# A convolution and mixture-of-experts kernel: the first tile's chain, the fillers, and the place of a conditional

## The chip, the cores and the metric

The kernel runs on one core of a Trainium2 chip. The metric is the device time of one execution in microseconds (us). A core has five engines that run their own instruction streams and wait for each other by semaphores: TensorE (PE, with its weight loads PEld), VectorE (DVE), ScalarE (ACT), GpSimd (POOL) and SyncE (SP), which here only issues transfers. Transfers by DMA run beside them.

## The reference

The input `x` has 8 x 256 tokens of 512 elements. Two stages follow, each with a residual:

```python
def _L0_xattn_ref(v, k, bias, x1, x2, num_heads):      # v = layernorm(x); x1 = x2 = ctx
    vr, x1r, x2r = (a.reshape(B, H, 8, L) for a in (v, x1, x2))         # H = 32
    kv = vr[:, :, :, None, :] * x2r[:, :, None, :, :]
    y = irfft(rfft(kv, n=2 * L) * rfft(k, n=2 * L), n=2 * L)[..., :L]   # causal convolution by head
    y = y + kv * skip
    return einsum('bhijl,bhil->bhjl', y, x1r).reshape(B, D, L)

x = x + _L0_xattn_ref(layernorm(x), ...)
x = x + ffn(layernorm(x))      # shared expert of 704, and the best 2 of 8 experts of 352
```

All of it is in float32. `ffn` is a gated network: `silu(x @ wg.T) * (x @ wu.T) @ wd.T`, for every token with the shared weights, and for each token with its two picked experts, weighted by their scores.

## The kernel before

**Convolution.** Tokens are laid out as 16 tiles of 128 rows (8 batches by 16 rows), two heads to a tile, 32 heads in all. For each head POOL forms the products `kv` in four blocks of 128x512 (`make_kv`), PE convolves them with the head's Toeplitz matrix (`conv_products`), and DVE weighs and sums the result. Each tile's rows are first normed and transposed (`vT`), later tiles a long way ahead through memory. Tiles 0 and 1 have no time for that: `first_of_all` norms them on the spot and `make_vT` transposes them on PE, whence ACT copies them out of PSUM. While tile 0's data are on their way, PE multiplies a block of zeros (`filler`, 128x256, `WARM` times); the result isn't used.

The chain of tile 0 before its first convolution is thus: `x` lands; DVE takes mean and variance; ACT the root (which needs the constant `eps`, written by POOL at L240); DVE the reciprocal and the product of mean and reciprocal; ACT the norm; PE four transposes; ACT one copy; POOL the first `kv` block; PE. ACT must load a table of function values before its first root. At L425 the first head takes `kv[:, 0]` three times before it needs the other blocks.

The order of the work is written out by hand in the program; each engine runs its instructions in the order in which they stand there. A loop over the heads (L892) makes one head's `kv` two heads ahead, and steps of the shared expert are spread over the later heads.

**Experts.** Routed tokens are sorted into blocks of 128 rows, each of one expert. There can be up to `NBLK` = 39 blocks; `NSURE` = 36 are always run, and the last three only if the count `more`, which the kernel itself computes and every engine loads into a register, exceeds 36. With these inputs it doesn't. For a block `k`: POOL gathers the rows (`gather`, four indirect DMAs), DVE transposes them (`block_T`), PE multiplies them by the gate and up weights (`block_up`), ACT and DVE form the hidden rows, DVE transposes these in 16 pieces (`block_hT`), PE multiplies by the down weights (`block_down`), ACT scales, and POOL adds the rows into the output with an indirect DMA. Each such scatter waits until the one before has landed, since two may add into the same row. PE reads the block's expert number into a register (`load_ek`, L1040). In `blocks`, gathers run four blocks ahead, the transposed rows two, and `block_down` two behind. The last block's hidden rows are transposed on PE (`last_hT`).

The conditional (`tc.If`, L1190) comes after all 36 blocks. Each engine has a compare and branch there. On the way that is not taken into the body an engine waits until it has finished what it was given, and moves its semaphores on by as much as the body would have; on POOL this also means a wait for all of its DMAs and an instruction INC_SWDGE_SEM.

Of the kernel before, what the change touches and what calls it, by code (L numbers as in the profile page):

```python
# [8 lines left out]
F32 = mybir.dt.float32  # L9
I32 = mybir.dt.int32  # L10
AF = mybir.ActivationFunctionType
ALU = mybir.AluOpType
# [45 lines left out]
H9 = 10  # L58
EPS = 1e-5
CTXBUFS, TZBUFS = 5, 3  # L60
WARM = 6
SCALE = 2.5


# [1 line left out]
def tile_xattn_moe(  # L66
# [74 lines left out]

    ones = const.tile([P, P], F32, name="ones")
    G.memset(ones, 1.0)
    filler = rows.tile([P, 2 * P], F32, tag="xg", name="filler")
    G.memset(filler, 0.0)
    ident = const.tile([P, P], F32, name="ident")
# [121 lines left out]
    def normed(xn, src, rb):  # L268
        A.activation(xn, src, AF.Identity, scale=rb[0], bias=rb[1])
# [5 lines left out]
        A.copy(dst, pt)  # L275

    vT, convT, xfT, xn1, xn2 = {}, {}, {}, {}, {}

    def make_vT(t):
        vT[t] = cvp.tile([P, NLB, B, R], F32, tag="vT", name=f"vT_{t}")  # L280
# [585 lines left out]
    def first_of_all(t):  # L866
        mv = small.tile([P, V.BN_AGGR_DIM], F32, tag="mv", name=f"mvp_{t}")
        stats(mv, f"p_{t}", x1[t])
        xn1[t] = cvp.tile([P, L], F32, tag="xn1", name=f"xn1_{t}", bufs=2)
        normed(xn1[t], x1.pop(t), rstd_of(mv, f"p_{t}"))  # L870

    first_of_all(0)

    warm = ps_acc.tile([P, 2, L], F32, tag="acc", name="warm")[:, 0, : 2 * P]
    for _ in range(WARM):
        T.matmul(warm, lhsT=ones, rhs=filler, start=True, stop=True)
    make_vT(0)
    make_kv(0)
    first_of_all(1)
    skip_products(0)  # L880
    make_kv(1)

    todo = iter(steps)
    done = 0
# [7 lines left out]
    for h in range(H):  # L892
        t, odd = divmod(h, 2)

        load_toeplitz(h + 2)
        if not odd:
            load_tile(t + 3)
            load_residual(t - 1)
        elif t == NT - 1:
            load_residual(t)  # L900
        if h == 3:
            load_shared()


        if odd and t + 2 < NT:
            first_root(t + 2)
        c, r = divmod(h - 10, 8)
        if c >= 0 and r == 2:
            route_scores(c)
        settle()  # L910
        pss = conv_products(h)
        if h > 1 and not odd:
            skip_turn(t)
        if not odd:
            first_sums(t + 2)
        elif t + 2 < NT:
            first_norm(t + 2)
            quarters(("v", t + 2), xv_d[t + 2])


        nine, picks_here = h >= H9, c >= 0 and r == 2
        if not nine:
            weigh(h, 0, pss[0])
        if odd and t > 0:
            add_residual(t - 1)
            mv = small.tile([P, V.BN_AGGR_DIM], F32, tag="mv", name=f"mv_{h}")
            stats(mv, f"2_{t}", x2[t - 1])
            rt = root(f"2_{t}", mv[:, 1:2], 1.0)
            V.reciprocal(rt, rt)
            nb = small.tile([P, 1], F32, tag="nb", name=f"nb2_{t}", bufs=3)  # L930
            V.tensor_scalar(nb, mv[:, 0:1], rt, -1.0, ALU.mult, ALU.mult)
            second_norm(t - 1, (rt, nb))
            quarters(("f", t - 1), xn_d[(t - 1) * P : t * P, :])
        if not odd and t > 0:
            add_skip(t - 1)
            if t + 1 < NT:
                square_vT(t + 1)
            if t > 1 and not picks_here:
                square_xfT(t - 2)
        if picks_here:  # L940
            route_pick(c)
        if c >= 0 and r == 4:
            route_places(c)
        if nine:
            weigh(h, 1, pss[1])
            weigh(h, 0, pss[0])
            if picks_here:
                square_xfT(t - 2)
        else:
            weigh(h, 1, pss[1])  # L950
        if odd or h == 0:
            skip_sum(t + odd)
        if h == 0:
            skip_turn(0)
        if h == 0:
            make_vT(1)

        if not odd:
            skip_spread(t)
        make_kv(h + 2)  # L960
        if not odd:
            skip_products(t + 1)

        while done < h - 9 + h // (H - 1) and steps[done][0] <= h:
            settle()
            step()

        if not odd and t > 0:
            residual_T(t - 1)
        if c >= 0:  # L970
            if r == 0:
                route_logits(c)
            if r == 1:
                route_T(c)
            if r == 3:
                route_ranks(c)
# [47 lines left out]
    def gather(k):  # L1024
        if k >= NBLK:
            return
        xgs[k] = rows.tile([P, NQ, P], F32, tag="xg", name=f"xg_{k}")
        for c in range(NQ):
            G.indirect_dma_start(  # L1029
                out=xgs[k][:, c, :],  # L1030
                out_offset=None,
                in_=xn_q,
                in_offset=bass.IndirectOffsetOnAxis(ap=src[:, c, k : k + 1], axis=0),
                bounds_check=(NTOK + P) * NQ - 1,
                oob_is_err=True,
            )
# [8 lines left out]
    def block_T(k):  # L1045

        if k >= NBLK:
            return
        xTs[k] = rows.tile([P, NLB, NQ, Q], F32, tag="xT", name=f"xT_{k}", bufs=3)
        V.transpose(  # L1050
            xTs[k].rearrange("p k c b -> p c k b"),
            xgs.pop(k).rearrange("p c (k a) -> p c k a", a=Q),
        )
# [22 lines left out]

    blk = pool("blk", 3, reuse_waits="tile")
    ps_b = pool("ps_b", 2, space=PS, reuse_waits="tile")
    NF = len(F_TILES)
    hs, hTb = {}, {}  # L1080

    def block_up(k, last):
        n = min(k + 1, NEXP)
        ps = ps_b.tile([P, 2, L], F32, tag="up", name=f"up_{k}")
        wk = wgu_sb[:, :n].rearrange("p e f -> p (e f)")
        for m in range(2):
            for j in range(NLB):
                T.matmul(  # L1088
                    ps[:, m, :FF],
                    lhsT=xTs[k][:, j].rearrange("p c b -> p (c b)"),  # L1090
                    rhs=wk[:, bass.ds(eks[k] * NGU + (m * NLB + j) * FF, FF)],
                    start=(j == 0),
                    stop=(j == NLB - 1),
                )
        hk = blk.tile([P, FF], F32, tag="h", name=f"h_{k}")
        A.activation(hk, ps[:, 0, :FF], AF.Sigmoid)  # L1096
        V.tensor_tensor(hk, hk, ps[:, 0, :FF], ALU.mult)  # L1097
        xTs.pop(k)
        if not last:
            V.tensor_tensor(hk, hk, ps[:, 1, :FF], ALU.mult)  # L1100
            hs[k] = hk
            return

        hp = blk.tile([P, NF, NQ, Q], F32, tag="hp", name=f"hp_{k}", bufs=1)
        for q0, q1, n in ((0, NQ - 1, NF), (NQ - 1, NQ, NF - 1)):
            squares = slice(q0 * NF * Q, (q0 * NF + (q1 - q0) * n) * Q)
            V.tensor_tensor(
                hp[:, :n, q0:q1].rearrange("p t q a -> p q t a"),
                hk[:, squares].rearrange("p (q t a) -> p q t a", t=n, a=Q),
                ps[:, 1, squares].rearrange("p (q t a) -> p q t a", t=n, a=Q),  # L1110
                ALU.mult,
            )
        hs[k] = hp
# [11 lines left out]
    def block_hT(k):  # L1125

        hk = hs.pop(k)
        hT = blk.tile([P, NF, NQ, Q], F32, tag="hT", name=f"hTb_{k}")
        for c in range(NQ):
            for q in range(NQ):  # L1130
                n = min(NF, FF // Q - q * NF)
# [7 lines left out]

    def block_down(k):  # L1140
        n = min(k + 1, NEXP)
        ps = ps_b.tile([P, L], F32, tag="dn", name=f"y_{k}")
        wk = wd_sb[:, :n].rearrange("p e f -> p (e f)")
        hT = hTb.pop(k)
        for ft, (_, fw) in enumerate(F_TILES):
# [4 lines left out]
                start=(ft == 0),  # L1150
                stop=(ft == NF - 1),
            )
        y = blk.tile([P, L], F32, tag="y", name=f"ys_{k}", bufs=3)
        A.activation(y, ps, AF.Copy, scale=gate[:, k : k + 1])  # L1154
        G.indirect_dma_start(  # L1155
            out=out,
# [5 lines left out]
            compute_op=ALU.add,  # L1162
        )

    def blocks(first, end):
        for k in range(first, end):
            if k + AHEAD < end:
                load_ek(k + AHEAD)
                if k > first:
                    block_T(k + AHEAD)  # L1170
            if k + AHEAD + 2 < end:
                gather(k + AHEAD + 2)
            if k < end - 1:
                block_up(k, False)
                block_hT(k)
                if k - 2 >= first:
                    block_down(k - 2)
            else:
                block_down(k - 2)
                block_up(k, True)  # L1180
                block_down(k - 1)
                last_hT(k)
                block_down(k)

    more = nc.values_load(
        used[0:1, 0:1], min_val=NEXP, max_val=NBLK,
        skip_runtime_bounds_check_because="the rows fill at most so many blocks",
    )
    blocks(0, NSURE)
    with tc.If(more > NSURE):  # L1190
        for k in range(NSURE, NBLK):
            gather(k)
        for k in range(NSURE, NBLK):
            block_T(k)
            if k < NSURE + AHEAD:
                load_ek(k)
        blocks(NSURE, NBLK)


def _orders():  # L1200
# [85 lines left out]
```

## Time and profile before

| | us |
|---|---|
| three runs: median (lowest to highest) | 799.49 (794.74 to 799.99) |
| the profiled execution | 795.8 |
| its span, first to last instruction | 794.1 |
| busy in the span: PE / DVE / POOL / ACT | 767.9 / 535.3 / 472.6 / 203.1 |
| a block of the expert loop on PE: up and down product | 4.90 and 2.74, 7.31 apart |
| last PE instruction ends | 777.2 |
| last scatter is issued | 781.3 |

The profile shows one execution. An engine is busy while an instruction of its own is at work; waits, register work and branches don't count. Names such as `kv<-vT,ctxT` give what an instruction writes and reads, `x4` says how many are merged into a line, and the bracket tells how long the engine stood idle before and who ended that. The granted clock of PE is a share of full speed. Matmuls of float32 are two passes each, so they are counted twice.

### The profile page before, as it was taken

To read this page: it belongs to the slowest core of one execution; us is meant where nothing else is said; L and a number is where in the kernel's file an instruction comes from. 1 tells how busy PE (TensorE), PEld (TensorE's weight loads), DVE (VectorE), ACT (ScalarE), POOL (GpSimd) and SP (SyncE) were. 2 spreads that over 40 slices of the span, in tenths; PEclk is the share of its full clock that TensorE was granted. 3 is DMA by queue.
4 is the path that set the end of the run, shared out by engine and by line. 5 is a ranking of instruction groups with operands and counts; after the bars stand their busy time and mean duration, and the time that the engine had idled before them with its cause. 6 is when DMAs were issued, how large, how long until landed. Compare 5 with 4: busy or idle time off the path is not lost. (4 is left out here: it accounts for less than half of the span.)

```text
span 794.1 us, 8485 instructions
## 1 busy us (share of the span) xinstructions
PE 767.9 (97%) x2379; PEld 353.8 (45%) x2379; DVE 535.3 (67%) x1209; ACT 203.1 (26%) x381; POOL 472.6 (60%) x474
## 2 busy tenths in 40 slices
PE   7999999999999999999999999999999999999991
PEld 4333333443333443433443444455555555555550
DVE  2768867768557768557766263288877877887750
ACT  2222254344144335135313210011111111111110
POOL 7767793469372559462640042766778777777421
PEclk9999999999999999999999999999999999999996
DMA  6495434234413234312100690395443444344332
GB/s 232 121 323 205 152 113 139 88 53 140 144 48 120 77 83 140 112 48 87 46 27 27 279 369 23 105 282 116 76 74 68 76 75 74 68 77 73 61 40 27
DMA packets 52142, 89.10 MB, mean 112 GB/s; under 512 B 8832, under 2 KB 24064, under 8 KB 50944
## 3 DMA queue, kind: packets, MB, share of 16 engines
q1 hardware_dynamic: 36960, 61.77, 24.1%
q0 software_dynamic: 10816, 18.92, 13.9%
q10 hardware_dynamic: 4320, 7.87, 2.7%
q8 instruction: 21, 0.34, 0.2%
q14 instruction: 25, 0.20, 0.1%
HBM read 66.34 MB, written 22.18 MB: 111 GB/s over the span
## 5 line engine op out<-in xcount | busy, mean ns | idle before, releaser
L402 PE MATMUL cv<-kv,tz 128*64 128x512 f32 (+2 forms) x720 | 192.0, 609 | 1.8 <-POOL kv L362 1.8
L1029 POOL DMA_INDIRECT xg<-xn_d,src x144 | 146.8, 1020 | 56.6 <-issue 39.1
L1088 PE MATMUL up<-wgu_sb,xT 128*128 (+1 forms) x576 | 176.1, 459 | 1.4 <-DVE x L743 1.4
L674 PE MATMUL gu<-xfT,wsh 128*128 128x512 f32 x352 | 155.0, 593 | 1.6 <-issue 1.6
L1132 DVE STREAM_TRANSPOSE hTb<-h 32x96 f32<-32x96 f32 (+1 forms) x560 | 146.3, 261 | 8.2
L362 POOL TENSOR_TENSOR kv<-vT,ctxT 128x512 f32<-128x512 f32 x128 | 132.5, 1067 | 15.0 <-PE cv L402 4.8
L1088 PEld LDWEIGHTS up<-wgu_sb,xT 128*128 128x128 f32 x576 | 109.2, 190 | 72.0 <-issue 15.6
L402 PEld LDWEIGHTS cv<-kv,tz 128*64 128x64 f32 (+2 forms) x720 | 61.4, 150 | 122.3 <-issue 98.5
L674 PEld LDWEIGHTS gu<-xfT,wsh 128*128 128x128 f32 x352 | 66.5, 190 | 85.0 <-issue 83.8
L1146 PE MATMUL y<-wd_sb,hTb 128*128 (+3 forms) x216 | 98.6, 593 | 0.8 <-ACT hTb L1121 0.8
L464 DVE TENSOR_TENSOR prod<-cv,ctxT 128x1024 f32<-128x1024 f32 x64 | 78.1, 1221 | 17.6 <-PE cv L402 15.9
L648 POOL DMA_INDIRECT table<-entries,to x32 | 31.8, 994 | 90.4 <-DVE at L644 81.9
L1155 POOL DMA_INDIRECT out_dram<-ys,row x36 | 58.2, 1616 | 45.0 <-ACT ys L1154 21.3
L473 DVE TENSOR_REDUCE convT<-prod 128x128 f32<-128x1024 f32 x64 | 78.1, 1220 | 2.2
L718 PE MATMUL dn<-wshd,hT 128*128 128x512 f32 x160 | 70.2, 593 | 0.0
L1146 PEld LDWEIGHTS y<-wd_sb,hTb 128*128 128x128 f32 (+1 forms) x216 | 41.0, 190 | 43.1 <-issue 34.7
L1096 ACT ACTIVATE h<-up 128x352 f32<-128x352 f32 x36 | 16.7, 464 | 165.6 <-PE up L1088 165.6
L518 POOL TENSOR_TENSOR skip<-ctxT,w 128x512 f32<-128x512 f32 x16 | 17.7, 1106 | 65.7 <-ACT w L510 36.5
L688 ACT ACTIVATE sg<-gu 128x512 f32<-128x512 f32 (+1 forms) x24 | 14.3, 596 | 164.6 <-PE gu L674 164.6
L1097 DVE TENSOR_TENSOR h<-h,up 128x352 f32<-128x352 f32 x36 | 18.6, 517 | 42.8 <-ACT h L1096 42.8
L402 PE MATMUL cv<-kv,td 128*128 128x512 f32 x88 | 47.2, 618 | 0.0
L718 PEld LDWEIGHTS dn<-wshd,hT 128*128 128x128 f32 x160 | 30.2, 190 | 37.6 <-issue 37.6
(145 smaller groups left out, 603.4 us busy)
## 6 DMA issues: line engine op xcount, KB each, us to landing
tz<-in_toep_dram SPq DMA_DIRECT2D x32, 384.0 KB, 3.4
wgu_sb<-in_egu_dram SPq DMA_DIRECT2D x8, 1408.0 KB, 16.3
ctxT<-in_cT_dram SPq DMA_DIRECT2D x16, 384.0 KB, 4.7
x<-in_xv_dram SPq DMA_DIRECT2D x16, 256.0 KB, 3.6
x<-in_x_dram SPq DMA_DIRECT2D x16, 256.0 KB, 4.8
xn_d<-xn ACTq DMA_DIRECT2D x16, 256.0 KB, 2.4
out_dram<-x SPq DMA_DIRECT2D x16, 256.0 KB, 2.4
wd_sb<-in_ed_dram SPq DMA_DIRECT2D x8, 512.0 KB, 10.8
```

What stands on the lines that cost most here:

```text
L362: G.tensor_tensor(kv[:, mb], vT[t][:, at, :, cols].unsqueeze(2).to_broadcast([P, B, NH, NH]), ctxT[t][:, at, :, cols].unsqueeze(3).to_broa ...
L402: T.matmul(banks[lb][cols], lhsT=w, rhs=x, start=first, stop=left[lb][here[0]] == 0,)
L464: V.tensor_tensor(prod, ps.rearrange("p k b j i -> p (k b) j i"), ctxT[t][:, 2 + 2 * n : 4 + 2 * n, :, cols] .rearrange("p k b i -> p (k b ...
L473: V.tensor_reduce(convT[t][:, two, :, cols].rearrange("p k b j -> p (k b) j"), prod, AX.X, ALU.add)
L648: ins = G.indirect_dma_start(out=table, out_offset=bass.IndirectOffsetOnAxis(ap=to[:, i : i + 1], axis=0), in_=entry[:, i, n, :], in_offse ...
L674: T.matmul(ps, lhsT=wsh[:, k, m0 : m0 + m], rhs=rhs[k], start=(k == 0), stop=(k == NLB - 1))
L718: T.matmul(ps, lhsT=hTs[c][:, ft, i * P : (i + 1) * P], rhs=wshd[:, ft, :], start=(ft == 0), stop=False,)
L1029: G.indirect_dma_start(out=xgs[k][:, c, :], out_offset=None, in_=xn_q, in_offset=bass.IndirectOffsetOnAxis(ap=src[:, c, k : k + 1], axis=0 ...
L1088: T.matmul(ps[:, m, :FF], lhsT=xTs[k][:, j].rearrange("p c b -> p (c b)"), rhs=wk[:, bass.ds(eks[k] * NGU + (m * NLB + j) * FF, FF)], star ...
L1132: V.transpose(hT[q * Q : (q + 1) * Q, :n, c], hk[c * Q : (c + 1) * Q, q * NF * Q : (q * NF + n) * Q].rearrange("p (t a) -> p t a", a=Q),)
L1146: T.matmul(ps, lhsT=hT[:fw, ft].rearrange("p c b -> p (c b)"), rhs=wk[:fw, bass.ds(eks[k] * NWD + ft * L, L)], start=(ft == 0), stop=(ft = ...
L1155: G.indirect_dma_start(out=out, out_offset=bass.IndirectOffsetOnAxis(ap=row[:, k : k + 1], axis=0), in_=y, in_offset=None, bounds_check=NT ...
```

## The change

At the start: ACT applies a root to a constant of one column as soon as that is written, so that the table is loaded there. Tiles 0 and 1 are normed in one DVE instruction from mean and reciprocal root, instead of a small DVE product and an ACT instruction. Tile 0's transposed rows are copied out of PSUM in three instructions, that of the block which the first `kv` reads ahead of the others. Five fillers instead of six stand before tile 0's transposes, and three more after them. On POOL the second head's `kv` is made before the skip products of tile 0, and the third head's before the spreading of tile 0's skip.

At the end: the conditional moves from behind the 36 blocks to before block 18. Its body runs the three extra blocks one after the other, without working ahead, in buffers of its own (`spare`, `ps_spare`). The loop's last blocks are in another order: `block_down` of block 32 and of block 33 each stand before the next `block_up`, so that from block 33 on the down products follow closer behind.

```diff
-WARM = 6
+WARM, FILL = 5, 3
@@ constants
+    A.activation(const.tile([P, 1], F32, name="table_first"), ones[:, :1], AF.Sqrt)
@@ beside make_vT
+    def make_first_vT():
+        vT[0] = cvp.tile([P, NLB, B, R], F32, tag="vT", name="vT_0")
+        xn = xn1.pop(0)
+        pt = ps_tp.tile([P, NLB, P], F32, tag="tp", name="ptv_0")
+        for mb in range(NLB):
+            k = BIN.index(mb)
+            T.transpose(pt[:, k, :], xn[:, k * P : (k + 1) * P], ident)
+        first = BIN.index(0)
+        for at in slice(first, first + 1), slice(0, first), slice(first + 1, NLB):
+            A.copy(vT[0][:, at].rearrange("p k b r -> p k (b r)"), pt[:, at])
@@ first_of_all
-        normed(xn1[t], x1.pop(t), rstd_of(mv, f"p_{t}"))
+        r = root(f"p_{t}", mv[:, 1:2], 1.0)
+        V.reciprocal(r, r)
+        V.tensor_scalar(xn1[t], x1.pop(t), mv[:, 0:1], r, ALU.subtract, ALU.mult)
@@ before the loop over the heads
-    for _ in range(WARM):
-        T.matmul(warm, lhsT=ones, rhs=filler, start=True, stop=True)
-    make_vT(0)
+    def fill(n):
+        for _ in range(n):
+            T.matmul(warm, lhsT=ones, rhs=filler, start=True, stop=True)
+    fill(WARM)
+    make_first_vT()
+    fill(FILL)
     make_kv(0)
     first_of_all(1)
+    make_kv(1)
     skip_products(0)
-    make_kv(1)
@@ in the loop over the heads
+        if h == 0:
+            make_kv(2)
         if not odd:
             skip_spread(t)
-        make_kv(h + 2)
+        if h > 0:
+            make_kv(h + 2)
@@ the blocks: gather, block_T, block_up, block_hT, block_down (one shown; alike in each)
-        xgs[k] = rows.tile([P, NQ, P], F32, tag="xg", name=f"xg_{k}")
+        xgs[k] = (rows if k < NSURE else spare).tile([P, NQ, P], F32, tag="xg", name=f"xg_{k}")
...
-    def blocks(first, end):
-        for k in range(first, end):
-            if k + AHEAD < end:
-                load_ek(k + AHEAD)
-                if k > first:
-                    block_T(k + AHEAD)
-            if k + AHEAD + 2 < end:
-                gather(k + AHEAD + 2)
-            if k < end - 1:
-                block_up(k, False)
-                block_hT(k)
-                if k - 2 >= first:
-                    block_down(k - 2)
-            else:
-                block_down(k - 2)
-                block_up(k, True)
-                block_down(k - 1)
-                last_hT(k)
-                block_down(k)
...
-    blocks(0, NSURE)
-    with tc.If(more > NSURE):
-        for k in range(NSURE, NBLK):
-            gather(k)
-        for k in range(NSURE, NBLK):
-            block_T(k)
-            if k < NSURE + AHEAD:
+    def rest_of_blocks():
+        with tc.If(more > NSURE):
+            for k in range(NSURE, NBLK):
+                gather(k)
                 load_ek(k)
-        blocks(NSURE, NBLK)
+                block_T(k)
+                block_up(k, False)
+                block_hT(k)
+                block_down(k)
+
+    last = NSURE - 1
+    for k in range(NSURE):
+        if k == NSURE // 2:
+            rest_of_blocks()
+        if k + AHEAD < NSURE:
+            load_ek(k + AHEAD)
+            if k > 0:
+                block_T(k + AHEAD)
+        if k + AHEAD + 2 < NSURE:
+            gather(k + AHEAD + 2)
+        block_up(k, k == last)
+        if k < last:
+            block_hT(k)
+        if 2 <= k < last - 1:
+            block_down(k - 2)
+        if k >= last - 2:
+            block_down(k - 1)
+    last_hT(last)
+    block_down(last)
```

More of the change, by code (lines that the diff above doesn't have):

```diff
@@ L1048, in block_T @@
             return
-        xTs[k] = rows.tile([P, NLB, NQ, Q], F32, tag="xT", name=f"xT_{k}", bufs=3)
+        own = (rows, 3) if k < NSURE else (spare, 1)
+        xTs[k] = own[0].tile([P, NLB, NQ, Q], F32, tag="xT", name=f"xT_{k}", bufs=own[1])
         V.transpose(
@@ L1078, in tile_xattn_moe @@
     ps_b = pool("ps_b", 2, space=PS, reuse_waits="tile")
+    spare = pool("spare", reuse_waits="tile")
+    ps_spare = pool("ps_spare", space=PS, reuse_waits="tile")
     NF = len(F_TILES)
@@ L1083, in block_up @@
         n = min(k + 1, NEXP)
-        ps = ps_b.tile([P, 2, L], F32, tag="up", name=f"up_{k}")
+        ps = (ps_b if k < NSURE else ps_spare).tile([P, 2, L], F32, tag="up", name=f"up_{k}")
         wk = wgu_sb[:, :n].rearrange("p e f -> p (e f)")
@@ L1094, in block_up @@
                 )
-        hk = blk.tile([P, FF], F32, tag="h", name=f"h_{k}")
+        hk = (blk if k < NSURE else spare).tile([P, FF], F32, tag="h", name=f"h_{k}")
         A.activation(hk, ps[:, 0, :FF], AF.Sigmoid)
@@ L1127, in block_hT @@
         hk = hs.pop(k)
-        hT = blk.tile([P, NF, NQ, Q], F32, tag="hT", name=f"hTb_{k}")
+        hT = (blk if k < NSURE else spare).tile([P, NF, NQ, Q], F32, tag="hT", name=f"hTb_{k}")
         for c in range(NQ):
@@ L1141, in block_down @@
         n = min(k + 1, NEXP)
-        ps = ps_b.tile([P, L], F32, tag="dn", name=f"y_{k}")
+        if k < NSURE:
+            ps = ps_b.tile([P, L], F32, tag="dn", name=f"y_{k}")
+        else:
+            ps = ps_spare.tile([P, 2, L], F32, tag="up", name=f"y_{k}")[:, 0]
         wk = wd_sb[:, :n].rearrange("p e f -> p (e f)")
@@ L1152, in block_down @@
             )
-        y = blk.tile([P, L], F32, tag="y", name=f"ys_{k}", bufs=3)
+        y = (blk if k < NSURE else spare).tile([P, L], F32, tag="y", name=f"ys_{k}")
         A.activation(y, ps, AF.Copy, scale=gate[:, k : k + 1])
```

## The prediction

> **What bounds the kernel now.** I read the busy table first. TensorE works 767.9 of 794.1 us, so only some 26 us can be won without taking matmuls away, and the question is where those 26 us lie.
>
> ```profile
> PE 767.9 (97%) x2379; PEld 353.8 (45%) x2379; DVE 535.3 (67%) x1209; ACT 203.1 (26%) x381; POOL 472.6 (60%) x474
> ```
>
> PE's gaps in order of time: 1.32 us before the first filler, 0.94 and 1.82 us in the first tile's chain, about 1.6 us at 105 us, 0.7 + 0.7 + 1.4 us around the routing, 0.8 us before the last block's product, and then nothing at all from 777.2 to 794.1: 16.9 us of tail. So the two ends matter, and I read both by the timeline (start us, duration us, engine, line, operation).
>
> ```profile
> 1.32 5.14 PE L876 MATMUL warm<-filler,ones 128*128 128x256 f32 x12 [1.32 <-POOL filler L145]
> 4.44 1.28 ACT L244 ACT_TABLE_LOAD   x1 [4.44 <-DVE mvp L237]
> 4.90 0.11 POOL L240 MEMSET eps<- 128x1 f32 x1
> 6.46 0.81 ACT L269 ACTIVATE xn<-x,nbp,rstdp 128x512 f32<-128x512 f32 x1 [0.42 <-DVE nbp L265]
> 7.41 0.63 PE L274 MATMUL ptv<-ident,xn 128*128 128x128 f32 x4 [0.94 <-ACT xn L269]
> 8.08 0.59 ACT L275 COPY vT<-ptv 128x512 f32<-128x512 f32 x1 [0.81 <-PE ptv L274]
> 8.75 4.13 POOL L362 TENSOR_TENSOR kv<-vT,ctxT 128x512 f32<-128x512 f32 x4 [3.74 <-ACT vT L275]
> 9.87 9.95 PE L402 MATMUL cv<-kv,tz 128*128 128x512 f32 x28 [1.82 <-POOL kv L362]
> ```
>
> The first convolution starts at 9.87 us, at the end of a serial chain. It also starts cold. In the windows of 2 us (busy time of each engine, then the granted clock) the clock falls to half just there:
>
> ```profile
> 8.00:10.00 2.00, 0.18 (x2) 0.14 (x1) 1.16 (x4) 0.88 (x2) 1.25 (x2) 0.85 0.98 301
> 10.00:12.00 2.00, 2.00 (x3) 0.97 (x4) 0.85 (x1) 1.11 (x2) 2.00 (x3) 0.50 1.07 394
> 12.00:14.00 2.00, 2.00 (x5) 0.77 (x5) 0.00 (x0) 1.33 (x5) 2.00 (x2) 0.80 0.99 372
> ```
>
> The tail: POOL's last output scatters, then the instructions at the lines of the conditional and of the program's end (duration min/median/max in ns, first and last start in us).
>
> ```profile
> 764.38 1.55 POOL L1155 DMA_INDIRECT out_dram<-ys,row  x1 [5.75 <-ACT ys L1154]
> 770.04 1.55 POOL L1155 DMA_INDIRECT out_dram<-ys,row  x1 [4.12 <-issue]
> 775.76 1.55 POOL L1155 DMA_INDIRECT out_dram<-ys,row  x1 [4.17 <-issue]
> 781.30 1.55 POOL L1155 DMA_INDIRECT out_dram<-ys,row  x1 [3.99 <-issue]
> L1190 POOLq EVENT_SEMAPHORE  x4: 17/42/4786, 781.3 to 786.2; - x4
> L1190 POOLq INC_SWDGE_SEM  x1: 1492/1492/1492, 786.3 to 786.3; - x1
> L1281 POOLq DRAIN  x3: 46/107/5411, 787.9 to 793.8; - x3
> ```
>
> Each scatter adds into the output and waits until the one before has landed, so the last four stand 5.64 us apart although their data came earlier (the last `ys` was ready at 777.93). After the last scatter, at 781.30, come 4.8 us of landing, 1.5 us of INC_SWDGE_SEM, 5.4 us of POOL's drain and 0.75 us of barriers: 12.7 us. Landing and barriers are owed anyway; INC_SWDGE_SEM belongs to the conditional's untaken branch.
>
> **The change part by part.** *The first chain.* The table load (1.28) moves to the start, where ACT idles. The root then waits for `eps`, which POOL still writes at 4.90 to 5.01: root at about 5.06 instead of 5.74, a gain of 0.68 and not 1.28. Root 0.29, reciprocal 0.16 and hops put the one-step norm at 5.58. The trace has no such DVE operation; the nearest row is the 128x512 SBUF copy at L827, 0.43 us, and as upper bound the 128x512 tensor_tensor rows, 0.69. I take 0.43, as it reads one tensor like the copy. So `xn` is ready at 6.01 instead of 7.27 (5.58 + 0.69 gives 6.27). Ten filler passes end by about 5.8, ahead of it. Transposes 6.15 to 6.78; the copy of the first block alone, an estimate of 0.25 us from the 128x256 copy at 0.364 and the 128x512 one at 0.586; POOL's first `kv` block at 7.15, and PE at 8.27: 1.6 us earlier. `ctxT` and `tz` of this tile have landed by then (4.7 and 7.7 us in the semaphore records).
>
> *The three further fillers* are six passes, 0.21 us each at full clock: they end near 8.1, ahead of the first `kv` block, so they cost nothing if the clock is up; at half clock they end at about 9.4 and take back 1.1. They fill the gap. Before, the convolution's first four issues took 9.87 to 13.13 (3.26 us) where 4 x 0.43 would do: 1.54 us lost. By the row the loss follows the idle 8.04 to 9.87, and the fillers save all of it. [...] I take it whole[...]. The reordered `kv` blocks keep POOL ahead: `kv` of head 2 no longer stands behind the skip's spreading (1.08 us), and the second head's block behind 2.5 us of skip products; head 2's block row on PE took 3.85 us where head 3's took 2.89, of which I count 0.15 back. Norm of tile 1: the DVE instruction there took 969 ns beside POOL's `kv` against 159 in tile 0, so the one-step norm may wait 1 us; its reader on PE comes 7 us later. Sum of the start: 1.6 + 1.54 + 0.15 = 3.3 us, and PE carries it through, since it is dense from there.
>
> *The conditional in mid loop, PE.* It stands before block 18. PE must retire block 15's down product, do two semaphore steps (51 ns each), branch, and reload its expert register (301 ns) before it may issue: some 1.2 us of idle, where before the sequencer ran ahead. ACT and DVE have slack (DVE waits 1.08 us a block for ACT).
>
> *The conditional, POOL.* Ahead of the branch stands block 15's scatter, at 641.52 before; behind it stand block 22's four gathers (643.44 before) and every later gather and scatter. POOL now waits for the landing (to 646.5), passes three waits and INC_SWDGE_SEM (1.49): gathers at 648.6, 5.2 us late. Who waits? Block 22's transposition on DVE, at 657.1 before; the gathers' data come at about 655.2. No one. But POOL doesn't catch up: four gathers and a scatter fill 7.24 us of a block's 7.31. So scatter 29 falls at 648.6 + 5.3 + 13 x 7.24 = 748.0 instead of 742.9. From there on scatters alone remain, 5.64 apart: the last at 748.0 + 6 x 5.64 = 781.85, against 781.30: 0.55 lost. The new order of the last blocks (block 32's down product one block earlier) would by itself let the chain start sooner, 757.06 + 4 x 5.7 = 779.9, plus PE's 1.2: 781.1. So both PE's stall and this gain are hidden under POOL's lag.
>
> *The tail.* INC_SWDGE_SEM is gone from the end. If the 5.41 us drain was its doing, landing 4.8 + waits 0.8 + barriers 0.75 = 6.35 us remain; if a drain costs that after any scatter, it now overlaps the landing: 1.55 + 5.4 + 0.75 = 7.7. I take the middle, 7.05, instead of 12.7: 5.65 gained.
>
> Sum: 3.3 - 0.55 + 5.65 = 8.4 us, 1.06%. The profiled execution took 795.8 us (span 794.1), 3.7 below the median of 799.49; made against it the sum gives 787.4, against the median 791.1. The latter is my forecast.
>
> [...] POOL's COMPARE_BRANCH took 53 ns and its next instruction came 0.14 us later. By the row a branch is nearly free; [...] I follow the row; the skipped bodies are of like length.
>
> **Rivals.** (1) *The drain's 5.4 us is work that INC_SWDGE_SEM leaves to POOL*, and the next gather must wait for it. For: the drain follows it at once, and the drain near the program's start is short. Against: the waiting SP saw the semaphores by 787.8. Then POOL's lag is 10.6 us, still within DVE's and PE's slack (block 20's transposed hidden rows are ready at 664.4 and read at 672.8), but the scatter chain ends 5.4 later, with 6.35 behind it: 3.3 - 5.95 + 6.35 = 3.7 us gained, 795.8. (2) *The start doesn't deliver*: [...] the fillers run at half clock and hold PE, about 0.5 us in place of 3.3: 793.9. (3) *Slower*: the drain is paid twice, once by POOL in mid loop, because the scatters queue behind it, and again after the last scatter with the tail as long as before: 3.3 - 5.95 + 0 = -2.65, 802.1. It decides as soon as POOL's extra delay and the tail together exceed 12.7 + 3.3 - 0.55 = 15.45 us; I count 7.05.
>
> **How the numbers follow.** Forecast 0.50, rival 1 0.27, rival 2 0.14, rival 3 0.09. The range runs from 786 (best tail, full start, against the profiled execution) to 797.5 (rival 1 with the slower norm and a cold start in part), and leaves out rival 3 and the edges. A measurement of this kernel can tell about 1% from no change; the forecast lies just beyond it, so six in ten of its chance count as faster, and little of the rivals: faster 0.34, same 0.60, slower 0.06.
>
> **What would show it.** First convolution matmul near 8.3 us at granted clock 1.0; a PE gap of about 1.2 us before block 18; in mid loop INC_SWDGE_SEM, and the gather after it within 0.5 us (forecast) or 5.5 us later (rival 1); scatter 29 about 5 us later relative to PE; last scatters 5.6 us apart to the end; 6 to 8 us from the last scatter to the end. Wrong if PE waits for gathers after block 18, if the tail stays at 12 us, or if the branch takes microseconds on PE.

## The result, and the profile after

Eight runs of the changed kernel have a median of 791.44 us (789.39 to 794.53); eight runs of the kernel before 799.55 us (794.74 to 800.49). The ratio is 0.9915, with a 95% interval from 0.9886 to 0.9944: 6.8 us less, between 4.5 and 9.1. Single executions of one kernel differ by some 5 us, and most of that goes with PE's clock: over the eight runs of the changed kernel, time and mean granted clock (0.989 to 0.995) correlate at -0.87, with 0.77 us to each 0.001 of clock.

The profiled execution took 791.86 us, its span is 790.1, against 795.8 and 794.1 before. First its busy table, as far as the engines go:

```profile
PE 768.2 (97%) x2383; PEld 353.7 (45%) x2383; DVE 535.1 (68%) x1209; ACT 201.8 (26%) x382; POOL 472.7 (60%) x474
```

The work is the same but for the fillers: the 4.0 us come out of PE's gaps. The timeline of the start (start us, duration us, engine, line, operation, idle time before it and who ended it):

```profile
5.04 0.29 ACT L246 ACTIVATE rstdp<-mvp,eps 128x1 f32<-128x1 f32 x1 [2.73 <-POOL eps L242]
5.57 0.55 DVE L886 TENSOR_SCALAR xn<-x,mvp,rstdp 128x512 f32<-128x512 f32 x1
6.26 0.63 PE L288 MATMUL ptv<-ident,xn 128*128 128x128 f32 x4 [0.99 <-DVE xn L886]
6.73 1.46 PE L894 MATMUL warm<-filler,ones 128*128 128x256 f32 x6
6.93 0.71 ACT L291 COPY vT<-ptv 128x128 f32<-128x128 f32 x3 [1.59 <-PE ptv L288]
7.28 6.43 POOL L376 TENSOR_TENSOR kv<-vT,ctxT 128x512 f32<-128x512 f32 x6 [2.27 <-ACT vT L291]
8.40 5.14 PE L416 MATMUL cv<-kv,tz 128*128 128x512 f32 x12 [0.21 <-POOL kv L376]
```

The root waits for `eps`, as the bracket says, and the first convolution starts at 8.40 instead of 9.87. The three fillers count as six matmuls, the four transposes as four. In the windows of 2 us (busy time of each engine, then PE's granted clock) it now runs at full clock, where before the clock stood at 0.50 from 10 to 12:

```profile
8.00:10.00 2.00, 1.79 (x5) 0.87 (x5) 0.65 (x2) 0.00 (x0) 2.00 (x3) 1.00 0.76 116
10.00:12.00 2.00, 2.00 (x6) 0.82 (x5) 0.00 (x0) 0.72 (x2) 2.00 (x3) 1.00 1.06 406
12.00:14.00 2.00, 2.00 (x9) 0.62 (x9) 0.00 (x0) 1.02 (x3) 2.00 (x3) 1.00 1.05 411
```

The same operations of PE come 2.9 us earlier than before from 18 us on, and 2.8 to 3.3 earlier up to 483 us. Then this execution loses part of the lead again, by a stretch at half clock:

```profile
484.00:486.00 2.00, 2.00 (x13) 1.44 (x13) 1.90 (x7) 0.00 (x0) 0.00 (x0) 0.93 0.00 0
486.00:488.00 2.00, 2.00 (x4) 0.91 (x3) 1.42 (x7) 0.00 (x0) 1.33 (x2) 0.50 0.00 0
488.00:490.00 2.00, 2.00 (x4) 0.72 (x3) 0.00 (x0) 0.00 (x0) 1.70 (x2) 0.72 0.26 66
```

The clock is at half from 485.73 to 489.14, for 3.41 us, behind a gap in the routing, a place that the change doesn't touch, and the lead shrinks from 2.83 us to 1.13, by 1.7 us, which is half of this stretch. In the profile of before the clock there is 1.00 (482 to 494). So the two profiles, set one against the other, understate the start's worth by 1.7 us. After the conditional's stall (0.86, below) and shorter gaps PE's last instruction ends only 0.06 us earlier than before (777.09 and 777.15): nearly all of the 3.9 us between these two spans lies behind it.

The conditional in mid loop. First the scatters of blocks 15 and 16 before the change, then PE and POOL with it:

```profile
641.52 1.62 POOL L1155 DMA_INDIRECT out_dram<-ys,row  x1 [0.30 <-issue]
648.74 1.63 POOL L1155 DMA_INDIRECT out_dram<-ys,row  x1 [0.30 <-issue]
```

```profile
638.71 5.00 PE L1116 MATMUL up<-wgu_sb,xT 128*128 x16 [0.86 <-PEq L1064]
640.45 1.62 POOL L1186 DMA_INDIRECT out_dram<-ys,row  x1 [0.30 <-DMA xg<-xn_d,src]
647.52 1.05 POOL L1053 DMA_INDIRECT xg<-xn_d,src  x1 [5.46 <-issue]
652.82 1.63 POOL L1186 DMA_INDIRECT out_dram<-ys,row  x1 [0.30 <-issue]
```

and the instructions of the conditional's line (duration min/median/max in ns, first and last start):

```profile
L1202 PEldq COMPARE_BRANCH  x1: 369/369/369, 631.6 to 631.6; - x1
L1202 POOLq COMPARE_BRANCH  x1: 53/53/53, 638.7 to 638.7; - x1
L1202 POOLq INC_SWDGE_SEM  x1: 871/871/871, 645.5 to 645.5; - x1
```

PE stands for 0.86 us. POOL stands behind block 15's scatter for 5.46 us, and block 16's scatter follows 12.37 us after it, where these two stood 7.22 apart before, and most others 7.24. The gather starts 1.15 us after INC_SWDGE_SEM has ended (646.37 to 647.52), and no drain stands between them. The tail, by POOL's last scatters and by its drain:

```profile
763.79 1.55 POOL L1186 DMA_INDIRECT out_dram<-ys,row  x1 [3.82 <-ACT h L1124]
769.27 1.55 POOL L1186 DMA_INDIRECT out_dram<-ys,row  x1 [3.94 <-issue]
774.71 1.55 POOL L1186 DMA_INDIRECT out_dram<-ys,row  x1 [3.88 <-ACT hTb L1149]
780.14 1.55 POOL L1186 DMA_INDIRECT out_dram<-ys,row  x1 [3.89 <-issue]
```

```profile
L1314 POOLq DRAIN  x3: 46/113/9404, 779.9 to 789.9; - x3
```

The end comes 10.01 us after the last scatter's issue instead of 12.79. INC_SWDGE_SEM's 1.5 us have left the end, but the drain, 5.4 us before, now takes 9.4.

To compare ends of different runs I use two distances: from PE's last instruction to the issue of the last scatter (before 4.15, after 3.05), and from there to the end of the span (12.79 and 10.01; "tail" below). Their sum, less PE's stall of 0.86, gives what the end is worth: 16.94 - 13.06 - 0.86 = 3.0 us. The first distance varies between executions of the same end: six that have the conditional before block 18, the new order and the last scatter as it is (the changed kernel, "A wait for the last landing", and the four variants of the start below) have from 2.34 to 3.17, and the end alone has 3.78. So a few tenths of it in a single pair of profiles show nothing.

### The profile page after: what moved, and what is told of

Same layout as the page of the kernel before. It is cut to its first block, busy times and chain, and to the rows that moved or that the text cites. A ratio compares the mean times of both kernels' runs of the same rounds, so it can differ in the third digit from the quotient of the medians.

```text
span 790.1 us, 8491 instructions
## 1 busy us (share of the span) xinstructions
PE 768.2 (97%) x2383; PEld 353.7 (45%) x2383; DVE 535.1 (68%) x1209; ACT 201.8 (26%) x382; POOL 472.7 (60%) x474
## 5 line engine op out<-in xcount | busy, mean ns | idle before, releaser
L688 PE MATMUL gu<-xfT,wsh 128*128 128x512 f32 x352 | 156.7, 598 | 1.2 <-issue 1.2
```

Of the source, the lines that this page charges most:

```text
L688: T.matmul(ps, lhsT=wsh[:, k, m0 : m0 + m], rhs=rhs[k], start=(k == 0), stop=(k == NLB - 1))
```

## The experiments

The first four were timed several times on another chip, where every kernel ran some 9 us longer (before: 808.74 median of 54 runs). All four profiles taken there have PE waiting 5.8 to 10.5 us for DVE, at about 510 us, ahead of the first expert block, where the profiles of before and after, above, have 1.39, and 7 to 14 us of half clock behind that. Why was not found. It lies ahead of all that is compared here, and ratios there are against the kernel before on the same chip. The other eight are one profiled execution each, on further chips; they are read by distances inside the trace, not by their totals. All edits are shown against the changed kernel, by the lines that matter.

**The start alone.** The edits of the start (table, norm, first copy, fillers, order of `kv`), with the conditional and the last blocks as they were before.

```diff
-        if k == NSURE // 2:
-            rest_of_blocks()
...
+    blocks(0, NSURE)
+    with tc.If(more > NSURE):
...
+        blocks(NSURE, NBLK)
```

> The edits at the start alone; the loop of blocks and the conditional as before. Theory: PE's first convolution at 8.4 us with the granted clock at 1.0, a lead of 2.9 to 3.2 us over the kernel before that PE carries to the expert blocks, and the old tail (12.7 us after the last scatter): about 3.2 us less than before, give or take one half-clock window of 1.7 us in either. Rival (the start is given back at the next wait, the table of slots near 485 us): 0.5 to 1 us less.

Measured: ratio 0.9955 (0.9931 to 0.998), 3.6 us less (1.6 to 5.6), more than the rival's 0.5 to 1. First convolution at 8.39, tail 12.85.

**The end alone.** The kernel before with the conditional in mid loop and the new order of the last blocks; table, norm, copies, fillers and order of `kv` are the old ones.

```diff
-WARM, FILL = 5, 3
+WARM = 6
...
-    fill(WARM)
-    make_first_vT()
-    fill(FILL)
+    for _ in range(WARM):
+        T.matmul(warm, lhsT=ones, rhs=filler, start=True, stop=True)
+    make_vT(0)
```

> The conditional in mid loop and the new order of the last blocks alone; the start as before. Theory: POOL is 5.1 us late after the conditional and stays so, the last scatter falls 0 to 0.5 us later than before, and the tail after it is 9.9 us instead of 12.7: about 2.5 us less than before. Rival (the start carries all of the gain, the tail's saving is eaten by POOL's lag): no difference.

Measured: ratio 0.9967 (0.9942 to 0.9991), 2.7 us less (0.7 to 4.7). Scatters 15 and 16 stand 12.26 apart, tail 9.65, PE's stall 0.86. Its start is the old one, with the first convolution at 10.00, and its windows show the old cold clock again:

```profile
10.00:12.00 2.00, 2.00 (x3) 0.97 (x4) 0.00 (x0) 1.26 (x2) 2.00 (x3) 0.50 1.05 401
12.00:14.00 2.00, 2.00 (x5) 0.84 (x4) 0.00 (x0) 1.29 (x5) 2.00 (x2) 0.67 1.05 410
```

The two parts together make 6.3 us, and the changed kernel as a whole 6.8. Each interval is some 2 us wide to either side, so the parts add up as far as these timings can tell, and no dependence of one on the other shows.

**The conditional before block 32 instead of 18.** There the last gather is already issued, so no gather stands behind it.

```diff
-        if k == NSURE // 2:
+        if k == NSURE - 4:
```

> The changed kernel with its conditional before block 32, where the gathers are over, instead of before block 18. Theory (POOL's lag from the conditional sets the last scatter): no lag at scatter 29, scatters 30 and 31 right behind their data, the last scatter bounded by the data of block 34 and one landing, 0.5 us earlier than with the conditional at 18; PE still stalls 0.9 us; the tail after the last scatter unchanged at 9.9. So 0.5 us less than the changed kernel, about 7.3 less than before. Rival (the place of the conditional matters through the drain, which counts from INC_SWDGE_SEM): the tail grows to 12 us or more, and the time by 2.

Measured: ratio 0.9939 (0.9914 to 0.9965), 4.9 us less than before. The scatters from 15 to 29 stay 7.31 apart, the distance from PE's end to the last scatter is 2.62, the tail 10.0. The rival, a longer tail, falls. The 0.43 us by which that distance is shorter than in the changed kernel isn't shown to be the place's doing, since four executions with the conditional before block 18 have 2.34 to 2.60. The timing is a miss: 4.9 instead of 7.3, with an interval too wide to tell this place of the conditional from that of the change. It isn't shown to be the better one.

**No conditional.** The three extra blocks are left out, which these inputs don't need.

```diff
-        if k == NSURE // 2:
-            rest_of_blocks()
```

> The changed kernel without the conditional; its body, the three extra blocks that these inputs don't need, is left out. Theory: no stall of 0.9 us on PE, no lag of POOL; the last scatter 1.35 us earlier than in the changed kernel; the tail still 9.9 us, since the drain follows the last scatter and has nothing to do with INC_SWDGE_SEM: 1.4 us less than the changed kernel, about 8.2 less than before. Rival (INC_SWDGE_SEM, wherever it stands, makes the last drain long): the tail falls to 6.4 us, 4.9 us less than the changed kernel.

Measured: ratio 0.9913 (0.987 to 0.9956), 7.0 us less. PE doesn't stall, no scatter lags, the distance from PE's end to the last scatter is 2.64, the tail 10.02. The changed kernel wasn't timed on this chip, so the forecast of 1.4 us against it stays untested; the profile shows 0.86 of it, PE's stall. The drain of this kernel, which has no INC_SWDGE_SEM in its loop or at its end:

```profile
L1312 POOLq DRAIN  x3: 46/113/9419, 789.6 to 799.5; - x3
```

It is as long as in the changed kernel, so its length isn't the conditional's doing.

**POOL later still.** Ten unneeded memsets on POOL behind the conditional.

```diff
+    late = spare.tile([P, L], F32, name="late")
...
+            for _ in range(10):
+                G.memset(late, 0.0)
```

> The changed kernel with ten memsets of 128x512 on POOL right after the conditional, 5.3 us more of lag. Theory (from the conditional on POOL runs at its own pace and sets the last scatter): block 16's scatter 17.7 us after block 15's instead of 12.4; no new gap on PE after the conditional's own 0.86; the last scatter 8.3 us after the last matmul's end instead of 3.05, all of the 5.3 us in the span. Rival (PE sets the end, the lag has room): the last scatter stays at about 3 us after the last matmul.

Measured, on POOL's and PE's timeline:

```profile
638.51 1.62 POOL L1187 DMA_INDIRECT out_dram<-ys,row  x1 [0.30 <-DMA xg<-xn_d,src]
644.84 5.76 POOL L1217 MEMSET late<- 128x512 f32 x10 [4.71 <-DMA out_dram<-ys,row]
650.89 1.06 POOL L1053 DMA_INDIRECT xg<-xn_d,src  x1 [0.29 <-DVE h L1126]
656.19 1.63 POOL L1187 DMA_INDIRECT out_dram<-ys,row  x1 [0.30 <-issue]
```

Scatters 15 and 16 are 17.68 apart, 5.31 more than in the changed kernel. PE shows no new gap: gathers that come 10 us late keep nobody waiting. But the distance from PE's end to the last scatter is 7.89 instead of 3.05. Of 5.31 us of extra lag 4.84 reach the end. The first 5.1 us, the conditional's own, had not: with the conditional left out the distance is 2.64, only 0.4 shorter than in the changed kernel. The reason is in the spacing. In the loop gathers and scatter fill 7.24 us of a block's 7.31, so POOL hardly catches up. Behind the last gather the scatters can follow each other at 5.2 to 5.9 us, and catch up with data that come every 7.3. In three of the start's variants below it has caught up by block 34, whose scatter waits for its data again (774.20 in the run without fillers, its data ready at 773.9). The slack is then used up, and what lag is added goes to the end, as the prediction's model of the chain has it.

**The old order of the last blocks**, with the conditional in mid loop.

```diff
+        if k == last:
+            block_down(k - 2)
...
-        if 2 <= k < last - 1:
+        if 2 <= k < last:
...
-        if k >= last - 2:
+        if k == last:
```

> The changed kernel with the last blocks in the old order (block 32's down product after block 34's up product). Theory (hidden under POOL's lag, but for block 32's data coming 0.7 us after the chain of scatters would take them): the last scatter 3.7 us after the last matmul's end instead of 3.05. Rival (the order carries the gain at the end): 1.4 us or more later, 4.4 and above.

Measured: distance from PE's end to the last scatter 3.87 instead of 3.05. Here block 32's rows are ready 7.3 us after block 31's and not 2.6, and its scatter, at 763.16, has to wait for them. The new order is worth 0.8 us between these two executions. Against the six with the new order, 2.34 to 3.17, it is 0.7 to 1.5, and against the end alone, 3.78, next to nothing: the direction is likely, the size is known roughly.

**A wait for the last landing.** One column of the last rows is overwritten by POOL after the scatter has landed, so that POOL's last work is a memset.

```diff
+        ylast[:] = [y]
...
+    G.memset(ylast[0][:, :1], 0.0)
```

> The changed kernel with a memset of one column on POOL after the last scatter, on the scattered tile, so that POOL waits for its landing before the drain. Theory (the drain counts from the last indirect DMA, whatever POOL does after): tail of 10.0 us from the last scatter as before. Rival (a drain takes 5.4 us from the last thing that POOL did, as it did after INC_SWDGE_SEM): landing 4.9, memset and wait 0.3, drain 5.4, barriers 0.75: 11.4 us.

Measured, by POOL's timeline and then by its drain:

```profile
779.87 1.55 POOL L1187 DMA_INDIRECT out_dram<-ys,row  x1 [3.88 <-issue]
784.84 0.10 POOL L1232 MEMSET ys<- 128x1 f32 x1 [3.41 <-DMA out_dram<-ys,row]
```

```profile
L1316 POOLq DRAIN  x3: 46/113/5546, 784.8 to 790.9; - x3
```

The tail is 11.33. My theory, 10.0, fell: it had the drain end a set time after the last indirect DMA, whatever POOL does later. The drain ends 5.43 us after the memset's end, although the scatter had landed before that. The drain of the kernel before ended 5.45 us after INC_SWDGE_SEM's end (787.82 to 793.27). So in these two kernels, where a short instruction came last, 5.4 us went by from its end.

**Without the last scatter.** Block 35's rows are missing in the output.

```diff
+        if k == NSURE - 1:
+            return
```

> The changed kernel without the last block's scatter, so that the rows of block 35 are missing in the output. Theory (the end is the last indirect DMA plus 10 us): block 34's scatter is the last and the span is 5.4 us shorter, with 10.0 us after it. Rival (what follows is bound to the end of the other engines' work): the tail after block 34's scatter is longer and less than 3 us are gained.

Measured: from PE's end to the end of the span 7.79 us instead of 13.06, so 5.3 less, the distance of one scatter. The tail behind what is now the last scatter is 9.89. PE's part is unchanged, so the end hangs on the chain of scatters. The rival, an end bound to the other engines, falls.

**No fillers behind the transposes.**

```diff
-WARM, FILL = 5, 3
+WARM, FILL = 6, 0
```

> The changed kernel with six fillers before tile 0's transposes and none after them. Theory (the fillers in the gap keep the clock up): PE idles about 1.4 us before the first convolution, which again starts at half clock, its first four issues taking some 3.3 us instead of 1.7; head 1's first matmul comes at 18.8 us instead of 17.3. Rival ([...] the fillers are needless): the first convolution at 8.4 to 8.6 us at clock 1.0, head 1's first matmul at 17.3 to 17.5.

Measured, PE's timeline and its window:

```profile
6.61 1.00 PE L288 MATMUL ptv<-ident,xn 128*128 128x128 f32 x4
9.12 5.14 PE L416 MATMUL cv<-kv,tz 128*128 128x512 f32 x12 [1.50 <-POOL kv L376]
```

```profile
10.00:12.00 2.00, 2.00 (x6) 0.95 (x5) 1.40 (x1) 0.20 (x1) 2.00 (x3) 1.00 1.05 398
```

I expected the convolution to start cold behind a gap of 1.50 us. It didn't: the clock is 1.00. The start at 9.12 comes from the other side of it. In this execution the clock rose late, at 7.43; the fillers ahead of the transposes, here six and not five, ended only at 6.6, 0.5 after the normed tile was ready, and the transposes took 1.00 us instead of 0.63. With five the fillers would have been over in time even at half clock (the sixth starts at 5.76, the tile is ready at 6.12), so part of the delay is this run's own extra filler. The gap by itself did not bring a cold convolution here. One execution can't say how often it does.

**The table loaded late**, as before.

```diff
-    A.activation(const.tile([P, 1], F32, name="table_first"), ones[:, :1], AF.Sqrt)
```

> The changed kernel without the early root, so that the table is loaded before tile 0's own root. Theory (eps, written at 5.0 us, bounds the root, so the early table is worth 0.7 and not 1.28): the root at 5.74 instead of 5.04, the first convolution at 9.1 instead of 8.4. Rival (another wait of the chain takes its place): the first convolution below 8.7.

Measured:

```profile
7.09 0.63 PE L287 MATMUL ptv<-ident,xn 128*128 128x128 f32 x4 [1.67 <-DVE xn L885]
9.22 5.14 PE L415 MATMUL cv<-kv,tz 128*128 128x512 f32 x12 [0.21 <-POOL kv L375]
```

The convolution starts 0.82 us later than in the changed kernel, not the table's 1.28: the root comes at 5.87 instead of 5.04, and the rest stays hidden behind `eps`. The rival falls. By 68.8 us, at the transposes behind the first tiles, 0.44 of it is left, and up to 483 us. There PE's wait for the table of slots is shorter in this execution and puts it 0.40 ahead, so what of the 0.82 lasts to the end isn't shown.

**The norm in two steps, on ACT**, as before.

```diff
-        r = root(f"p_{t}", mv[:, 1:2], 1.0)
-        V.reciprocal(r, r)
-        V.tensor_scalar(xn1[t], x1.pop(t), mv[:, 0:1], r, ALU.subtract, ALU.mult)
+        normed(xn1[t], x1.pop(t), rstd_of(mv, f"p_{t}"))
```

> The changed kernel with the norm of tiles 0 and 1 in two steps (a small DVE product, then ACT). Theory: the normed tile is ready 0.4 to 0.5 us later, the first convolution at 8.85 instead of 8.4. Rival (the DVE norm of 0.55 us is no shorter than product and ACT norm together): no more than 0.1 us of difference.

Measured, on PE:

```profile
6.72 1.09 PE L288 MATMUL ptv<-ident,xn 128*128 128x128 f32 x4 [0.76 <-ACT xn L271]
7.60 2.77 PE L892 MATMUL warm<-filler,ones 128*128 128x256 f32 x6
10.16 4.21 PE L416 MATMUL cv<-kv,tz 128*128 128x512 f32 x9
```

The transposes start 0.45 later, which is the norm's worth. The convolution is 1.76 later, against 0.45 expected: here too the clock rose late. Transposes (1.09 us) and fillers (2.77 us instead of 1.46) ran at half clock. POOL began its first `kv` at 8.19, 0.91 later than in the changed kernel, so PE could have had it at about 9.3; the fillers held PE until 10.16, some 0.85 us more. This is what the prediction's second rival spoke of, and the bracket that is missing at the convolution shows it: PE waited for nobody. The clock rose only at 10.53, so the convolution's first 0.37 us were at half clock as well.

**The old order of the first `kv` blocks on POOL.**

```diff
     first_of_all(1)
-    make_kv(1)
     skip_products(0)
+    make_kv(1)
...
-        if h == 0:
-            make_kv(2)
...
-        if h > 0:
-            make_kv(h + 2)
+        make_kv(h + 2)
```

> The changed kernel with POOL's products in the old order (skip products of tile 0 before head 1's blocks, skip spreading before head 2's). Theory (the earlier first convolution needs head 1's blocks earlier): the blocks of head 1 are done at 18.2 us where PE wants the last near 18.0, and head 2's are later by the spreading's 1.1 us: PE waits 0.5 to 1.5 us more in heads 1 and 2 together, so that head 3's first matmul is that much later than 34.7. Rival (POOL is ahead enough in either order): no difference.

Measured: first convolution at 8.40, as in the changed kernel; 0.42 us later at 26.9 us, 0.34 at head 3's first matmul (34.65), 0.13 at 68.8, and 0.51 ahead at 483. I had expected 0.5 to 1.5 at head 3. The new order is worth next to nothing that lasts.

## Why the prediction was right, and where it wasn't

**The sum.** Forecast 8.4 us, measured 6.8 by the ratio (4.5 to 9.1) and 8.1 between the medians. That 791.1 stands so near 791.44 is partly luck: by the parts the gain is 2.8 to 3.6 at the start (traces, and the start timed alone) and some 3 at the end (2.7 timed; 2.6 to 3.7 in the traces), 6 to 7 together. The start's term of 3.3 holds; the end's, 5.65 - 0.55 = 5.1, is 2.1 too large.

**The start.** Root at 5.04 for 5.06, bounded by `eps` and not by the table, as the run with the late table confirms. The norm took 0.55, between the 0.43 taken and the bound of 0.69. The first `kv` block began at 7.28 for 7.15, the convolution at 8.40 for 8.27: the difference is the norm's. The copy of the first block took 0.27 for 0.25.

The clock's 1.54 us was the weak term. I took it whole, an estimate from the one profile of before. Half-clock stretches amid the work last 3.41 us in the profiles of before (9.40 to 12.82) and after (485.73 to 489.14), and 3.4, 6.8, 10.2 or 13.7 us over all traces here; they fall on different places in different executions. With the old start both profiles, that of before and that with the end alone, have one on the first convolution (0.50 from 10 to 12 in each). With the changed start none of eight has: the clock first rises between 4.45 and 7.01 us, and the convolution starts at 8.39 to 8.75. Nor has the run without the gap's fillers (1.00). So the term came nearly whole (the first four issues took 1.82 us for 3.26, a gain of 1.44), yet not shown to be because the fillers filled the gap.

How much PE idles just before may be what counts; that is a guess from these traces. In the two old starts the clock fell again 3.41 us after it had risen (5.99 to 9.40, and 6.50 to 9.92), and PE was busy, by its rows, for 1.1 and 0.9 us of these. In the first 3.41 us after the rise it was busy for 1.9 without the gap's fillers, 1.7 with the late table and 2.4 or more in the eight, and the clock stayed. No amount of work that keeps the clock up comes out of this: in the routing the clock fell behind 3.41 us with 2.3 of work in the changed kernel, and stayed behind 1.5 in the end alone.

In two executions the late rise cost 0.7 and 1.8 us by another way (some of the former is the sixth filler, 0.45 of the latter the norm). That the fillers are of use has not been shown; that they can hold PE at half clock has. The 0.15 for the order of `kv` was nothing that lasted.

**The conditional.** PE's stall was 0.86 for 1.2. POOL's lag was 5.1 (12.37 less 7.24) for 5.2, in part by luck: INC_SWDGE_SEM took 0.87 instead of 1.49, but the gather came 1.15 us after it and not within 0.5. Scatter 29 fell at 746.90; block 15's was 1.07 earlier than before, and with that added back it is 747.97, forecast 748.0. The last scatters stand 5.4 to 5.8 apart, as forecast. The branch cost nothing but the stall: POOL's took 53 ns, as at the end of the kernel before, PE's 369 ns.

In all 13 profiles with a conditional a 16 KB transfer of the instruction queue starts 1.0 to 1.7 us after PE's branch and takes 0.9 to 1.3; the kernel without the conditional has one such transfer less. In the kernel before PE branched at 774.62, and the transfer ran from 775.72 to 776.68. In the changed kernel it runs from 632.67 to 634.01, while PE's sequencer, having branched at 631.58, goes on to its next instruction only at 637.89, when the last matmul before it is done. The transfer was over 3.9 us before that. So no wait for it shows on PE, whose sequencer was 6.3 us ahead, a lead that the prediction didn't count. What the branch costs without such a lead wasn't shown.

With PE's stall taken in, the last scatter came 0.24 us earlier (4.15 - 3.05 - 0.86) instead of 0.55 later; over the executions with this end it is between 0.95 earlier and 0.5 later. The new order, which I had hidden under POOL's lag, probably brings part of it.

**The tail was mis-sized.** I took 7.05, the middle between 6.35 (the drain is INC_SWDGE_SEM's doing) and 7.7 (a drain of 5.4 us follows the scatter's 1.55). Measured: 10.01. The first bound fell with the kernel that has no conditional. The second had the drain's 5.4 right and what it follows wrong: it is not the end of the scatter's row. From the semaphore records of the last scatter:

| | landed after its issue | drain ends after the landing | drain ends after the row's end |
|---|---|---|---|
| the end alone | 4.45 | 4.38 | 7.28 |
| the table loaded late | 4.59 | 4.38 | 7.42 |
| the changed kernel | 4.80 | 4.38 | 7.63 |
| no conditional | 4.82 | 4.37 | 7.65 |

In all eleven kernels in which the scatter is POOL's last work, the drain ends 4.3 to 4.4 us after the landing, while the distance to the row's end varies by 0.37. So the end follows the landing, which the prediction had let the drain overlap: 4.8 of landing, 4.4 and 0.8 of barriers make 10.0. Where a short instruction came after the landing, the drain ended 5.43 us after that, and 5.45 in the kernel before. One reading fits both: 5.4 us from POOL's last work, with that of a scatter over 1.0 to 1.1 us before its landing is reported. What POOL does after the 1.55 us of the scatter's row isn't shown, and this reading stays argued.

What the change took from the end is thus INC_SWDGE_SEM's 1.5, the short waits around it, and some 1.1 of the drain: 2.8 us. (The prediction's parts of the old tail, 4.8 + 1.5 + 5.4 + 0.75, make 12.45 and not 12.7; the trace has 12.79, with these waits.)

**The rivals.** That a later gather must wait for a drain fell at once: it came 1.15 us after INC_SWDGE_SEM, with no drain between. That the drain is paid twice fell with it; the kernel became faster. That the start fails through fillers at half clock didn't happen in the change's profile; fillers at half clock that held PE were seen in two others (by 0.5 us with six fillers ahead of the transposes, by some 0.85 us with the norm on ACT).

## What to carry to other kernels

When an instruction at the end of a program is long, ask what it would still wait for if the work ahead of it were gone. Its duration behind one predecessor need not be that behind another: POOL's drain took 5.4 us behind INC_SWDGE_SEM and 9.4 behind a scatter. The conditional, moved from the end into the loop, delayed POOL's whole later chain there, by 5.1 us, and costs what this chain cannot catch up by its end; so follow such an engine, not the busiest one, to its last instruction. PE's branch showed no wait for instructions with 6.3 us of work queued ahead of it; look for the instruction transfer behind a branch, and for the lead over it, before counting on that elsewhere. Fillers should be few enough to be over in time at half clock as well: the three behind the transposes took 1.46 us at full clock and 2.77 at half.

## What the hardware did that I had not expected

POOL's closing drain ended 5.4 us after a short instruction (5.45 in the kernel before, 5.43 with the wait for the landing), and 4.3 to 4.4 after the landing of an indirect DMA that adds into memory (eleven kernels, the drain 9.0 to 9.4 us long), with or without a conditional in the program. PE's untaken conditional was followed by a 16 KB instruction transfer in all 13 profiles that have one, over 0.5 us before PE's next instruction in the kernel before and 3.9 us before it in the changed one. One half-clock stretch of 3.41 us cost the changed kernel 1.7 us of its lead; one more or less of them is as large as most parts of this change. INC_SWDGE_SEM took 0.87 us in mid loop before block 18, 1.39 before block 32 and 1.49 at the end.
